# A two-layer convolution and GRU kernel: statistics of one image ahead of the blocks, the others beside them, and matrices built on four row tiles

## The chip, the cores and the metric

The kernel runs on one core of one Trainium2 chip. The time is device microseconds (us) of one execution. The engines of the core are TensorE (PE; PEld is its loading of weights), VectorE (DVE), ScalarE (ACT), GpSimd (POOL) and SyncE (SP). Each has its own queue of instructions[...]. DMAs are issued from the queues of SP, ACT and POOL.

## The reference, cut to what is computed

The input x is 4 images of 64 channels and 256 x 256 pixels in float32. Two layers follow each other, each on a normalised input (groups of two channels within an image) and with a residual.

```python
# layer 0
hidden = conv1x1(gn(x), w1); hidden = depthwise3x3(hidden, w_dw)
q, k, v = split(hidden, 3, axis=1)
out = irfft2(rfft2(patches8x8(q)) * rfft2(patches8x8(k)))
out = layernorm_over_channels(out) * ln_w + ln_b
x = x + conv1x1(v * out, w_out)
# layer 1: a GRU that walks over the 256 columns of gn(x)
x = x + gru_scan(gn(x), w_ih, w_hh, b_ih, b_hh)

def gn(v, G=32):      # mean and variance per image and group of 2 channels
    g = v.reshape(B, G, C // G, H, W)
    return ((g - mean(g)) / sqrt(var(g) + 1e-5)).reshape(v.shape)
```

The scalars of the first gn (one mean and one 1/sqrt(variance) for each image and group) need every pixel of that image before its first pixel can be normalised.

## The kernel before

It has four stages, all recorded through a small helper that keeps instructions in program order; so every instruction carries the helper's line, L156, in the profile, and tiles tell the groups apart.

**The start (lines 219 to 270).** Constants are loaded on ACT's queue. Then the matrices are built: depthwise convolution and transform together are linear, so for each of 384 hidden channels there is one matrix of 100 (a 10 x 10 patch with its border) by 64. It is a product of nine tap matrices (`bt`) with nine weights (`wd`): matmuls of 9 rows into PSUM (`psb`), in 16 groups of four with 256 columns and 16 groups of four with 128. ACT copies each group into the tile `t`, and POOL's queue writes three tiles to DRAM as `t_all`, 9.8 MB. Beside that, SP's queue loads x in 32 chunks `xc` of 2 MB, three buffers deep, and DVE takes eight `bn_stats` of 512 elements from each and aggregates them (`mv`). `group_norm_scalars` turns the means and variances of all images into `sc0`, with two small matmuls (against `avg`, which averages the two channels of a group), a Sqrt and sixteen copies.

**The blocks (lines 274 to 660).** 32 blocks `n`, eight to an image. For a block, POOL's queue loads the padded patches in four tiles `xq` of 800 KB (`load`), and `normalize` applies `sc0` of the image `n // 8` to them in place. Then in order:
- `pointwise(n, 0, ...)`: 16 units, each eight matmuls (`psring<-w_sb,xq`) and a copy into `h` by ACT, or by DVE for the units named in the call;
- `finish(n - 1)`: the gate, projection and residual of the block before, four units `u`; DVE adds the projection to the residual `xr` and takes `bn_stats` for layer 1, and SP stores `xr` in DRAM as `x1`. The last unit's projection is put off into the next step;
- `circular(n, 0, ...)`: for `sp` 0 to 3, `transform` of q and of k (64 matmuls `psring<-h,t`, the matrices `t` fetched by SP from `t_all`, four ahead), a copy of q by ACT, and the products `pr0`, `pr1` by DVE. After `sp` 2 an `inverse` (`psring<-pr,g_sb`) of the first two;
- `pointwise(n, 1, ...)`, `circular(n, 1, ...)` for the second half, beside which the layer norm of z (`layer_norm`, a generator advanced by `next(norm)`) takes its statistics on DVE;
- `pointwise(n, 2, ...)` and eight `values`, with `normalize` of block `n + 1`.

PSUM is one ring of eight banks (`psum()`), taken in turn. The work tiles q, k, pr0, pr1, y, xr and lnm share a pool `wk` of seven buffers: a tile gets a buffer that has come free and its first writer waits for the buffer's last readers.

**The turn to layer 1 (lines 667 to 681)** and **the GRU (683 to 836)** come last; the change touches only the load of `avg4` there.

Of the kernel before, what the change touches and what calls it, by code (L numbers as in the profile page):

```python
# [10 lines left out]
F32 = mybir.dt.float32  # L11
# [60 lines left out]
def tap_constants():  # L72
# [8 lines left out]
    return out.reshape(9, 128, HALO).astype(np.float32)  # L81


def group_norm_scalars(nc, pool, psum, avg, mv, eps, name):

    mean = pool.tile([P, NPAIR], F32, tag=f"{name}_mean", name=f"{name}_mean")
    rstd = pool.tile([P, NPAIR], F32, tag=f"{name}_rstd", name=f"{name}_rstd")  # L90
    m_c = pool.tile([P, NPAIR], F32, tag=f"{name}_mc", name=f"{name}_mc")
    d = pool.tile([P, NPAIR], F32, tag=f"{name}_d", name=f"{name}_d")
    nc.vector.tensor_copy(m_c, mv[:, :, 0])
    pm = psum.tile([P, NPAIR], F32, tag="gn", name=f"{name}_pm")
    nc.tensor.matmul(pm, lhsT=avg, rhs=m_c, start=True, stop=True)
    nc.vector.tensor_copy(mean, pm)
    nc.vector.tensor_tensor(d, m_c, mean, ALU.subtract)
    nc.vector.tensor_tensor(d, d, d, ALU.mult)
    nc.vector.tensor_tensor(d, d, mv[:, :, 1], ALU.add)
    pv = psum.tile([P, NPAIR], F32, tag="gn", name=f"{name}_pv")  # L100
    nc.tensor.matmul(pv, lhsT=avg, rhs=d, start=True, stop=True)
    nc.scalar.activation(rstd, pv, AF.Sqrt, bias=eps, scale=1.0)
    nc.vector.reciprocal(rstd, rstd)
    return mean, rstd
# [57 lines left out]
def tile_conv_then_gru(  # L162
# [26 lines left out]
    x_pair = x.rearrange("b c w h -> (b c) (w h)")  # L189
# [15 lines left out]

    wi = const.tile([P, 9, C], F32, tag="wi", name="wi")
# [11 lines left out]

    CH = 4096
    NST = W * H // 512  # L220
    with tc.tile_pool(name="xa", bufs=3) as xa, tc.tile_pool(name="sta", bufs=1) as sta, tc.tile_pool(
        name="gnps", bufs=1, space=PSUM
    ) as gnps, tc.tile_pool(name="bps", bufs=3, space=PSUM) as bps:
        avg = sta.tile([P, P], F32, tag="avg", name="avg")
        nc.scalar.dma_start(avg, avg2[0])
        wd = sta.tile([9, HID], F32, tag="wd", name="wd")
        nc.scalar.dma_start(wd, w_dw)
        ts = [sta.tile([HALO, P, NS], F32, tag=f"t{i}", name=f"t_{i}") for i in range(3)]
        for kind in range(2):
            bt = sta.tile([9, NS, HALO], F32, tag="bt", name=f"bt_{kind}")  # L230
            nc.scalar.dma_start(bt, taps[:, kind * NS : (kind + 1) * NS, :])
            for s in range(0, NS, 4):
                to = ts[0:2] if kind == 0 else ts[2:3]
                ps = bps.tile([HALO, 4, len(to) * P], F32, tag="b", name=f"psb_{kind}_{s}")
                for i in range(4):
                    nc.tensor.matmul(
                        ps[:, i, :],
                        lhsT=bt[:, s + i, :],
                        rhs=wd[:, 0 : 2 * P] if kind == 0 else wd[:, 2 * P : 3 * P],
                        start=True,  # L240
                        stop=True,
                    )
                for i, t in enumerate(to):
                    nc.scalar.copy(
                        t[:, :, s : s + 4], ps[:, :, i * P : (i + 1) * P].rearrange("p s c -> p c s")
                    )
        for i in range(3):
            nc.gpsimd.dma_start(
                t_all[i].rearrange("n p k -> p n k"), ts[i].rearrange("p (n c) k -> p n (c k)", n=8)
            )  # L250
# [641 lines left out]
```

## Time and profile before

| what | us |
|---|---|
| median of 3 runs (lowest, highest) | 5957.78 (5954.8, 5962.69) |
| the profiled execution, its own time | 5951.97 |
| its span, from first to last instruction | 5950.2 |
| first matmul of the blocks | 229.25 |
| issue of the four xq loads of block 0 | 215.66 |
| third write of t_all issued | 123.63 |
| first xq load of blocks 9, 10, 11 (one each block) | 1338.67, 1466.93, 1599.72 |
| busy: PE, DVE, ACT, POOL | 5537.8, 4085.5, 3465.8, 399.5 |

The three writes of `t_all` took 64.4, 80.3 and 114.1 us from issue to landing, while chunks of x were loaded beside them. In the profile a line of the timeline gives the start and the length in us, the engine, the operation, what it writes and reads with sizes, how many instructions of the kind were merged, and in brackets how long the engine had been idle and what ended that. In the rows of waits the numbers are us in total, how often, and the longest. "issue" is time in which the engine waited for nothing that the profile shows.

### The profile page before, as it was taken

To read this page: it belongs to the slowest core of one execution; us is meant where nothing else is said; L and a number is where in the kernel's file an instruction comes from. 1 tells how busy PE (TensorE), PEld (TensorE's weight loads), DVE (VectorE), ACT (ScalarE), POOL (GpSimd) and SP (SyncE) were. 2 spreads that over 40 slices of the span, in tenths; PEclk is the share of its full clock that TensorE was granted. 3 is DMA by queue.
4 is the path that set the end of the run, shared out by engine and by line. 5 is a ranking of instruction groups with operands and counts; after the bars stand their busy time and mean duration, and the time that the engine had idled before them with its cause. 6 is when DMAs were issued, how large, how long until landed. Compare 5 with 4: busy or idle time off the path is not lost.

```text
span 5950.2 us, 278865 instructions
## 1 busy us (share of the span) xinstructions
PE 5537.8 (93%) x127184; PEld 4770.7 (80%) x127184; DVE 4085.5 (69%) x9549; ACT 3465.8 (58%) x4617; POOL 399.5 (7%) x602
## 2 busy tenths in 40 slices
PE   5499999999999999999999999999979999999998
PEld 4478888888887888887888888888868888888887
DVE  7566776676676666676666767766666766676666
ACT  1256665666665656665565666565645555555555
POOL 0000000000000000000000000000002212122121
PEclk9999999999999999999999999999989999999999
DMA  9544545445445444444444554544444444444442
GB/s 384 213 133 144 139 132 147 121 141 144 140 126 142 137 135 141 140 134 133 143 124 138 146 144 123 149 131 132 128 119 113 113 113 113 113 112 113 111 113 80
DMA packets 549698, 817.79 MB, mean 137 GB/s; under 512 B 38443, under 2 KB 432436, under 8 KB 544404
## 3 DMA queue, kind: packets, MB, share of 16 engines
q1 hardware_dynamic: 523264, 683.80, 40.4%
q0 software_dynamic: 22320, 114.70, 5.8%
q8 instruction: 996, 16.32, 1.1%
q10 hardware_dynamic: 2934, 1.46, 0.1%
q14 instruction: 184, 1.51, 0.1%
HBM read 622.22 MB, written 144.05 MB: 129 GB/s over the span
## 4 chain that ended last, share of the span: by engine, by line
PE 64%; DVE 18%; ACT 7%; DMA 5%; issue 5%; SPq 0%; DVEq 0%; ACTq 0%; POOL 0%; POOLq 0%
PE psring L156 61%; DVE g L156 7%; DVE n L156 6%; DVE st L156 4%; ACT n L156 4%; DMA t<-t_all 2%; DMA xc<-in_x 2%; ACT v L156 2%; ACT z L156 1%; PE pshr L156 1%; PE pshz L156 1%; PE psni L156 1%; ACT h L156 1%; PE pshn L156 0%; SPq L156 0%
## 5 line engine op out<-in xcount | busy, mean ns | idle before, releaser
L156 PEld LDWEIGHTS psring<-h,t 100*32 100x32 f32 x40960 | 1336.1, 116 | 266.6 <-issue 184.8
L156 PE MATMUL psring<-h,t 100*32 100x128 f32 x40960 | 1437.4, 274 | 88.8 <-ACT h L156 35.6
L156 PEld LDWEIGHTS psring<-w_sb,xq 64*100 64x100 f32 x24576 | 1352.4, 163 | 86.1 <-issue 48.8
L156 PE MATMUL psring<-w_sb,xq 64*100 64x128 f32 x24576 | 1394.2, 271 | 27.3 <-POOL xq L156 17.8
L156 ACT COPY h<-psring 100x1024 f32<-100x1024 f32 x1274 | 1203.2, 1027 | 147.7 <-PE psring L156 140.9
L156 DVE TENSOR_TENSOR pr<-psring,q 128x512 f32<-128x512 f32 (+1 forms) x576 | 463.8, 860 | 338.6 <-PE psring L156 334.7
L156 DVE BATCH_NORM_STATS2 lnst<-z 128x6 f32<-128x64 f32 x4096 | 544.8, 212 | 118.7 <-ACT z L156 118.7
L156 DVE TENSOR_TENSOR z<-z,lnm 128x1024 f32<-128x1024 f32 x512 | 612.6, 1217 | 8.7
L156 ACT ACTIVATE n<-n,bias_sb 128x288 f32<-128x288 f32 (+7 forms) x510 | 259.8, 509 | 574.0 <-DVE n L156 574.0
L156 ACT COPY q<-psring 128x1024 f32<-128x1024 f32 x256 | 259.1, 1012 | 514.2 <-PE psring L156 457.6
L156 ACT COPY z<-psring 128x2048 f32<-128x2048 f32 x128 | 238.8, 1866 | 502.2 <-PE psring L156 485.1
L156 PE MATMUL psring<-pr,g_sb 32*64 32x512 f32 x8192 | 486.1, 598 | 7.2 <-issue 7.1
L156 ACT ACTIVATE y<-psring,ln_sb 128x512 f32<-128x512 f32 x512 | 372.1, 781 | 200.8 <-PE psring L156 197.2
L156 DVE COPY h<-psring 100x1024 f32<-100x1024 f32 x262 | 320.3, 1223 | 218.5 <-PE psring L156 216.2
L156 PE MATMUL pshr<-st,wi 64*64 64x144 f32 (+7 forms) x12240 | 433.3, 270 | 14.0 <-DVE st L156 13.4
L156 PE MATMUL psni<-st,wi 64*64 64x144 f32 (+7 forms) x12240 | 438.4, 270 | 8.0 <-issue 6.6
L156 DVE TENSOR_TENSOR g<-xn,n 128x288 f32<-128x288 f32 (+7 forms) x510 | 217.3, 426 | 325.2 <-ACT n L156 325.2
L156 PE MATMUL pshz<-st,wi 64*64 64x144 f32 (+7 forms) x12240 | 436.6, 269 | 1.8 <-issue 1.1
L156 DVE TENSOR_TENSOR y<-psring,y 128x1024 f32<-128x1024 f32 x256 | 312.3, 1220 | 122.7 <-ACT y L156 121.2
L156 POOL TENSOR_TENSOR raw<-raw,st 128x512 f32<-128x512 f32 x256 | 303.4, 1185 | 1208.1 <-DVE st L156 511.1
L156 PEld LDWEIGHTS pshr<-st,wi 64*64 64x64 f32 x12240 | 361.7, 133 | 17.0 <-issue 16.7
L156 PEld LDWEIGHTS psni<-st,wi 64*64 64x64 f32 x12240 | 361.5, 133 | 13.5 <-issue 9.9
(94 smaller groups left out, 6944.7 us busy)
## 6 DMA issues: line engine op xcount, KB each, us to landing
t<-t_all SPq DMA_DIRECT2D x768, 400.0 KB
xq<-in_xh POOLq DMA_DIRECT2D x128, 800.0 KB, 4.6
xc<-in_x SPq DMA_DIRECT2D x32, 2048.0 KB
xr<-in_x SPq DMA_DIRECT2D x256, 256.0 KB
x<-xr SPq DMA_DIRECT2D x256, 256.0 KB
raw<-x SPq DMA_DIRECT2D x128, 256.0 KB
raw<-x SPq DMA_DIRECT2D x256, 128.0 KB
xt<-xn SPq DMA_DIRECT2D x256, 128.0 KB
```

The source lines that it names most:

```text
L156: return self.tc.keep_in_program_order(got(*args, **kwargs))
```

## The change

The start takes the statistics of the first image only: eight chunks, each loaded as two halves of 64 partitions (`piece`: the image's upper and lower half of columns lie on the two halves of the partitions), with `bn_stats` into `bn0` and an aggregation into `st0` for each chunk. `norm_of_pieces` makes the scalars of one image from eight means and variances; it is a generator in three steps, and one matrix `avg2` serves everywhere.

In blocks 0 to 23 the next image is read in pieces beside the work: `look` loads 512 KB in two DMAs on POOL's queue into a work tile, `count` takes two `bn_stats` from it on DVE, four times in a block, and the fourth aggregates. In blocks 7, 15 and 23 `norm_of_pieces` is run at units 4, 8 and 12 of the third pointwise.

For the matrices, `bt` and `wd` are laid out on four groups of 32 partitions (nine rows of each used), so that the four matmuls of a group stand at four `tile_position`s and write four banks; ACT copies a group of 256 columns with one instruction. The loads of `wi`, `wh` and `bias_sb` stand after the scalars of the first image instead of ahead of everything.

```diff
-    avg = sta.tile([P, P], F32, tag="avg", name="avg")
...
+        bt = sta.tile([P, 32, HALO], F32, tag="bt", name="bt")
+        wd = sta.tile([P, HID], F32, tag="wd", name="wd")
+        for i in range(4):
+            nc.scalar.dma_start(bt[32 * i : 32 * i + 9], taps[i])
+            nc.sync.dma_start(wd[32 * i : 32 * i + 9], w_dw)
+        avg4 = sta.tile([P, 1024], F32, tag="avg4", name="avg4_0")
+        nc.sync.dma_start(avg4[:, 0:P], avg2)
+        ts = sta.tile([HALO, 3 * P, NS], F32, tag="ts", name="ts")
+        banks = bps.tile([P, 8, 512], F32, tag="b", name="psb")
+        for i in range(32):
+            kind, s = i // 16, i % 16
+            c0, num = 2 * P * kind, 2 * P - P * kind
+            ps = banks[0:HALO, 4 * (i % 2) : 4 * (i % 2) + 4, 0:num]
+            for k in range(4):
+                at = slice(32 * k, 32 * k + 9)
+                nc.tensor.matmul(
+                    ps[:, k],
+                    lhsT=bt[at, i, :],
+                    rhs=wd[at, c0 : c0 + num],
+                    start=True,
+                    stop=True,
+                    tile_position=(32 * k, 0),
+                )
+            nc.scalar.copy(ts[:, c0 : c0 + num, 4 * s : 4 * s + 4], ps.rearrange("p s c -> p c s"))
...
+        for i in range(8):
+            xc = xa.tile([P, 4096], F32, tag="xc", name=f"xc_{i}")
+            for at, of in piece(x, 0, i, 0, 16):
+                nc.sync.dma_start(xc[at], of)
+            for k in range(8):
+                nc.vector.bn_stats(bn0[:, k, :], xc[:, 512 * k : 512 * k + 512])
+            nc.vector.bn_aggr(st0[:, i, :], bn0)
+        for _ in norm_of_pieces(nc, st0, avg4, lambda: banks[:, 0, 0:1], eps, sc0[:, 0]):
+            pass
...
+def norm_of_pieces(nc, st, t, psum, eps, sc):
+    m_all, d, total, mean = t[:, 128:136], t[:, 136:144], t[:, 144:145], t[:, 145:146]
+    nc.vector.tensor_copy(m_all, st[:, :, 0])
+    nc.vector.tensor_reduce(total, m_all, mybir.AxisListType.X, ALU.add)
+    yield
+    pm = psum()
+    nc.tensor.matmul(pm, lhsT=t[:, 0:P], rhs=total, start=True, stop=True)
+    nc.vector.tensor_copy(mean, pm)
+    nc.vector.tensor_tensor(d, m_all, mean.to_broadcast([P, 8]), ALU.subtract)
+    nc.vector.tensor_tensor(d, d, d, ALU.mult)
+    nc.vector.tensor_tensor(d, d, st[:, :, 1], ALU.add)
+    nc.vector.tensor_reduce(total, d, mybir.AxisListType.X, ALU.add)
+    yield
+    pv = psum()
+    nc.tensor.matmul(pv, lhsT=t[:, 0:P], rhs=total, start=True, stop=True)
+    nc.scalar.activation(sc[:, 1:2], pv, AF.Sqrt, bias=eps, scale=1.0)
+    nc.vector.reciprocal(sc[:, 1:2], sc[:, 1:2])
+    nc.vector.scalar_tensor_tensor(sc[:, 0:1], mean, -1.0, sc[:, 1:2], ALU.mult, ALU.mult)
+    yield
...
+        def look(n, k, t):
+            for at, of in piece(x, n // 8 + 1, n % 8, 4 * k, 4):
+                nc.gpsimd.dma_start(t[at], of)
+
+        def count(n, k, t):
+            for i in range(2):
+                nc.vector.bn_stats(bn0[:, 2 * k + i, :], t[:, 512 * i : 512 * i + 512])
+            if k == 3:
+                nc.vector.bn_aggr(st0[:, n % 8, :], bn0)
...
-            circular(n, 0, lambda sp: None)
+            more = n // 8 + 1 < B
+            if more:
+                seen = work(f"seen0_{n}")
+                look(n, 0, seen)
+            circular(n, 0, lambda sp: count(n, 0, seen) if more and sp == 1 else None)
+            if more:
+                seen = work(f"seen1_{n}")
+                look(n, 1, seen)
             for unit in range(16):
                 pointwise(n, 1, unit, unit in (5, 8, 11, 14))
+                if more and unit in (8, 14):
+                    count(n, unit // 7, seen)
+                    look(n, unit // 7 + 1, seen)
             flush()
             norm = layer_norm(n)
-            circular(n, 1, lambda sp: next(norm))
+
+            def beside(sp):
+                next(norm)
+                if more and sp == 1:
+                    count(n, 3, seen)
+
+            circular(n, 1, beside)
+            image = None
+            if more and n % 8 == 7:
+                t = work(f"avg4_{n}")
+                nc.gpsimd.dma_start(t[:, 0:P], avg2)
+                image = norm_of_pieces(nc, st0, t, lambda: psum()[:, 0, 0:1], eps, sc0[:, n // 8 + 1])
             for unit in range(16):
                 pointwise(n, 2, unit, unit in (6, 14))
+                if image and unit in (4, 8, 12):
+                    next(image)
```

## The prediction

> **What bounds the kernel now.** I read the share of each engine over the whole span first, then stretches of the start, then the start and one block in order of time, and last what the TensorE (PE) waits for. The 40 slices:
>
> ```profile
> PE   5499999999999999999999999999979999999998
> DVE  7566776676676666676666767766666766676666
> DMA  9544545445445444444444554544444444444442
> ```
>
> After the first 1.5 slices (149 us each) PE is full until the end; DVE has about a third of its time free, but not evenly. At the start DMA is full and PE idle. Two stretches of the start (columns: busy us of PE, PEld, DVE, ACT, POOL; clock; DMA share; GB/s), then the timeline:
>
> ```profile
> 100.00:150.00 50.00, 22.72 (x107) 22.37 (x105) 41.95 (x65) 8.19 (x14) 1.00 (x1) 1.00 1.01 427
> 150.00:200.00 50.00, 0.00 (x0) 0.00 (x0) 38.69 (x65) 0.00 (x0) 0.00 (x0) 1.00 0.99 409
> ...
> 189.26 4.85 DVE L156 BATCH_NORM_STATS2 st<-xc 128x6 f32<-128x512 f32 x8 [1.42 <-DMA xc<-in_x]
> 200.68 4.84 DVE L156 BATCH_NORM_STATS2 st<-xc 128x6 f32<-128x512 f32 x8 [0.32 <-DMA xc<-in_x]
> 215.66 2.17 POOL L156 DMA_DIRECT2D xq<-in_xh  x4 [91.04 <-DMA t<-t_all]
> 229.25 6.51 PE L156 MATMUL psring<-w_sb,xq 64*100 64x128 f32 x64 [17.80 <-POOL xq L156]
> ```
>
> The reader sees: all 67 MB of x pass through DVE before the first useful matmul at 229.25 us, a chunk of 2 MB every 6.26 us (335 GB/s) while the matrices' writes share the DMA engines; a chunk costs DVE 4.85 us (0.605 us each of 8). From the issue of the xq loads to the first matmul it is 13.6 us. The statistics ahead of the blocks are thus the bound of the start, and PE of the blocks. In the steady part, from 1317 to 1445 us: products of a block's second half and its layer-norm statistics; then, in the next block, products of the first half around the residual of the block before, and a copy of the second pointwise stage:
>
> ```profile
> 1327.68 2.41 DVE L156 TENSOR_TENSOR pr<-psring,q 128x1024 f32<-128x1024 f32 x3
> 1346.31 5.46 DVE L156 BATCH_NORM_STATS2 lnst<-z 128x6 f32<-128x64 f32 x42
> ...
> 1410.07 2.42 DVE L156 TENSOR_TENSOR pr<-psring,q 128x1024 f32<-128x1024 f32 x3 [1.12 <-PE psring L156]
> 1412.41 1.28 DVE L156 TENSOR_TENSOR xr<-psring,xr 128x512 f32<-128x512 f32 x2
> 1415.56 2.42 DVE L156 TENSOR_TENSOR pr<-psring,q 128x1024 f32<-128x1024 f32 x3 [0.15 <-PE psring L156]
> 1419.06 1.23 DVE L156 TENSOR_TENSOR pr<-psring,q 128x1024 f32<-128x1024 f32 x1 [1.07 <-PE psring L156]
> 1437.42 1.23 DVE L156 COPY h<-psring 100x1024 f32<-100x1024 f32 x1 [1.40 <-PE psring L156]
> ```
>
> The brackets are DVE's slack: 1.12, 0.15 and 1.07 us around the first products, 1.40 us between pointwise copies, none at 1327.68. What PE waits for in blocks 1 to 30 (us in total, times, longest):
>
> ```profile
> PE psring L156 <- issue: 42.0, 40, 2.5
> PE psring L156 <- DMA t<-t_all: 7.6, 15, 1.0
> ```
>
> Fetches of the t matrices already come late now and then, so added DMA in the blocks isn't free.
>
> [...] in this trace the pointwise units, on two tiles of 64 rows, take 0.89 us for their eight matmuls of 128 columns (14.22 us for 16 units), so something does run side by side there.  [...] two queues share (335 GB/s of xc beside about 90 of t_all). [...]
>
> **The change part by part.**
>
> *Start.* Removed: 24 of 32 chunks of x. Left: 16.8 MB in 16 loads, 64 statistics and 8 aggregations. Those of 48 elements cost 0.37 us (the st<-bn row), so a chunk is 5.2 us of DVE. SP now issues four wd and one avg4 load first; I put the first chunk at 11 us. Eight chunks at 5.2 to 6.26 us end at 53 to 60 us, take 56. The new scalars have about ten DVE steps, two matmuls and a Sqrt instead of 13 more copies (209.22 to 215.25 took 6.0 us): 4.5 us, so 61 us.
>
> *Matrices.* bt now comes in four loads on ACT's queue behind five others; before, bt took 10.7 and 8.7 us to land under load. I take 19 us for the first matmul (14 to 22). Before, PE took 54.9 us for 16 groups of four 256-column matmuls and 27.6 us for 16 groups of 128 columns: 3.43 and 1.72 us a group. If four tiles run together it is a quarter, 0.86 and 0.43 us, and ACT is the slower: 1.03 us (the h row, of the same size) for 16 groups and 0.59 us (the t<-psb copies) for 16, 26 us in all. So the writes of t_all start at 36 and 45 us. Until 56 us they get 90 GB/s beside xc, about 1.8 MB of 9.8. The other 8 MB alone: [...] 20 to 30 us, so 76 to 86, take 80.5. xq (POOL) and the first t fetches wait for that landing and for the freed space, not for the statistics. Meanwhile ACT issues the 13 moved weight loads (0.65 us each plus lane waits, some 16 us before, 3.49 to 19.6) between 61 and 77, and b_rz on DVE waits for the last of them: hidden under the t_all writes; were those quicker, this would be next, at about 78. First matmul: 80.5 + 13.6 = 94 us. Gain 229.25 - 94 = 135 us, between 126 and 144.
>
> *Blocks 0 to 23, each.* Added: 8 loads of 256 KB on POOL's queue, 8 statistics (two take 1.29 us, bn<-xr row) and one aggregation, 5.5 us of DVE. Edit by edit:
> - Count 0, after the products of sp 1 (end 1417.98): 1.3 us into 1.07 us of idle; the products of sp 2 start 0.2 us late, and their bank is only needed by k of sp 3 after the inverse, over 2 us later. Nothing.
> - But the tile for it is one of the 7 work buffers. By the waits in the instruction order of the changed kernel, pr1 of sp 0 now gets the buffer whose last reader is the store of xr 2, which q of sp 1 got before. That store is issued at 1407.65 to 1408.9 and pr1 is due at 1411.3, 2.4 us later; all that the trace says of its landing is "before 1413.76". Delay of DVE 0 to 2.5 us, 1.4 taken; the inverse has 0.9 us of slack (1417.98 to 1418.93): 0.5 us lost, bounds 0 and 1.6.
> - Count 1 after the copy of unit 8: 1.3 in 1.40. Count 2 after unit 14: before 6.9 us of idle. Nothing. The load for count 2 starts when count 1 ends (1437.4) and is read at 1441.3 or, within that idle time, later[...]. POOL's queue holds behind these loads only xq loads, which are due later (1338.67 in the block shown).
> - Count 3 with the aggregation: 1.66 us into no idle at 1327.68, so the products end at 1331.75 instead of 1330.08; k of sp 3 on PE needs that bank after q of sp 3, at about 1331.75: 0.2 us lost.
> - DMA: 2 MB at 430 GB/s, 4.9 us of all engines per block, in four bursts, three beside transforms which prefetch t. Bounds 0 and 1.3 us (one burst in front of one fetch that has no slack), 0.5 taken.
> Sum 1.2 us, 29 us over 24 blocks; bounds 5 and 65.
>
> *Blocks 7, 15, 23.* The scalars' three steps stand in the third pointwise. The reading of the first matmul's result is in DVE's queue behind the 42 statistics (end 1351.77), and PE at unit 12 (about 1348.9) needs that bank and then the second matmul's operand, some five small DVE steps of 0.2 us later: PE waits 1348.9 to 1352.9, less the unit itself, 3.2 us. Three times: 10 us. PSUM's ring moves by four banks, which leaves its pattern alike.
>
> Sum: -135 + 29 + 10 = -96. The profiled execution took 5951.97 us (5950.2 span), giving 5856; the median of the runs shown stands 5.8 above it: 5862.
>
> **Rivals.**
> 1. All cover holds: matrices ready sooner (first matmul 86 us) and blocks pay 0.2 us each: -143 + 5 + 10 = -128, 5830. For it: DVE is idle a third of the time. Against: the fetches already late.
> 2. Half hidden: each block pays 3 us (store and fetches both on the path): -135 + 72 + 10 = -53, 5905. For it: DMA share 0.96 to 1.01 in the stretch 1404 to 1408, where the first look falls.
> 3. The four tiles don't overlap and the build doesn't do what it says: PE's 82.5 us replace ACT's 26, the third write starts at 101 us and ends at about 113 [...], first matmul 127: -102 + 39 = -63, 5895. For it: nothing here shows four tiles; against it: the two of 64 rows.
> 4. Slower: the store of xr 2, made of 512-byte pieces, [...] lands late, DVE's queue stands at pr1 of sp 0 and with it everything to the inverse. It decides from (135 - 10) / 24 = 5.2 us a block, a landing of 8.5 us after issue; the trace bounds it below 4.9 now. At 7 us a block: +43, 6001.
>
> **Numbers.** Forecast 0.66, rival 1 0.13, rival 2 0.08, rival 3 0.05, rival 4 0.06, and 0.02 for an end within 0.2% (12 us, what a measurement can tell from no change). Range 5826 to 5908: from rival 1 to rival 2 with their bounds. Faster 0.92, same 0.02, slower 0.06.
>
> **What would show it.** First w_sb,xq matmul at 86 to 103 us, released by the t_all landing, not by sc; a block of 24 lasting 129.3 us instead of about 128, the last eight unchanged; a PE wait of 3 us in blocks 7, 15, 23; DVE waiting for x<-xr at pr1. Wrong if xq waits for the statistics, or if PE waits for t grow by more than 2 us a block.

## The result and the profile after

| what | before | after |
|---|---|---|
| median (lowest to highest), 6 runs each, us | 5960.9 (5954.8 to 5975.34) | 5926.84 (5912.88 to 5938.16) |
| ratio, 95% interval | | 0.9938 [0.9926, 0.9951] |
| the profiled execution, its own time and span, us | 5951.97, 5950.2 | 5924.77, 5923.0 |
| first xq load, first matmul of the blocks, us | 215.66, 229.25 | 129.31, 140.37 |
| a block, mean of blocks 1 to 23, us | 129.07 | 130.86 |

The change is faster by 34 us (0.6 per cent) and not by the 96 us of the forecast's sum; 5926.84 lies above its range (5826 to 5908). Count a block from its first xq load to the next block's. Then the two spans compare piece by piece: the first xq load came 86.4 us sooner, block 0 took 2.8 us more, blocks 1 to 23 together 41.0 more, blocks 24 to 30 6.0 more, and what follows the first load of block 31 (its work, the turn to layer 1 and the GRU) 9.4 more. -86.4 + 2.8 + 41.0 + 6.0 + 9.4 = -27.2, the difference of the spans. Up to the first matmul of the blocks the start gave 88.9 us where 135 were forecast (140.37 us stands where 94 was expected), and everything behind it took 61.7 us more where 39 were forecast. The start is the larger part of the miss.

The page of after, three rows of the 40 slices:

```profile
PE   2999999999999999999999999999979999999998
DVE  2676776777667777776767776666766666676666
DMA  8455555555555555555555545444454444444442
```

The first digit of PE was 5 because the building of the matrices took long; now it is built quickly and PE stands idle for most of the slice all the same. DMA is at 5 instead of 4 in most slices of the blocks: the looks. Stretches of the start of after (columns: length, busy us of PE, clock, DMA share, GB/s):

```profile
20.00:30.00 10.00, 7.13 (x44) 1.00 0.96 202
40.00:50.00 10.00, 9.03 (x104) 1.00 1.02 215
80.00:90.00 10.00, 0.00 (x0) 1.00 1.01 286
110.00:120.00 10.00, 0.00 (x0) 1.00 0.68 187
120.00:128.00 8.00, 0.00 (x0) 1.00 0.28 68
```

The share and the bytes have to be read side by side. From 20 to 50 us the DMA engines are as busy as they were before, but they move 202 to 215 GB/s where the same share meant 409 to 427 GB/s before (from 100 to 200 us). At the end of the start they are busy for a quarter of their time only, and still neither PE nor DVE works. The timeline of after:

```profile
25.81 2.10 PE L157 MATMUL psb<-wd,bt 9*100 9x256 f32 x16 [0.25 <-ACT ts L157]
27.07 1.93 ACT L157 COPY ts<-psb 100x1024 f32<-100x1024 f32 x2 [0.40 <-PE psb L157]
27.67 0.37 DVE L157 BATCH_NORM_AGGREGATE st<-bn 128x2 f32<-128x48 f32 x1
37.01 0.37 DVE L157 BATCH_NORM_AGGREGATE st<-bn 128x2 f32<-128x48 f32 x1
...
54.94 1.00 POOL L157 DMA_DIRECT2D t_all<-ts  x1 [9.47 <-ACT ts L157]
...
97.48 0.37 DVE L157 BATCH_NORM_AGGREGATE st<-bn 128x2 f32<-128x48 f32 x1
...
128.52 7.54 SPq L157 DMA_DIRECT2D t<-t_all  x4
129.31 2.16 POOL L157 DMA_DIRECT2D xq<-in_xh  x4 [73.37 <-DMA wi<-in_w_ih]
140.37 5.21 PE L157 MATMUL psring<-w_sb,xq 64*100 64x128 f32 x64 [39.83 <-POOL xq L157]
```

An aggregation ends each chunk: they come about every 10 us, from 27.67 to 97.48, and DVE needs 4.84 us of that. So it is the loading that sets the pace now. The building runs well: two groups of four matmuls in 2.10 us, and the next two 2.32 us after them, with the two copies of ACT (1.93 us and a gap) as the pace: 1.16 us a group. The third write of `t_all` is issued at 54.94; from issue to landing the writes took 58.6, 81.7 and 73.5 us, while chunks of x were loaded beside them. The statistics and their scalars are done at 102.5, but the t fetch (SP's first loads of matrices from `t_all`) and the xq loads wait for the writes' landing: the third lands at 128.44. The bracket of the xq loads names a load of `wi`, because a wait for several things is put down to the one that came last. In a run below that loads `wi` much later, xq follows the landing just as closely (100.46 after 99.59 there, 129.31 after 128.44 here).

In the blocks, what PE waits for in after from 250 to 4100 us (us in total, times, longest):

```profile
PE psring L157 <- issue: 45.1, 49, 3.0
PE psring L157 <- DMA t<-t_all: 19.7, 30, 1.3
PE psring L157 <- DVE avg L157: 5.7, 3, 1.9
```

The same stretch of before has 39.0 us of issue, 7.6 us for t, and no avg. DVE in after, through blocks 1 to 23:

```profile
DVE pr L157 <- DMA x<-xr: 63.2, 23, 3.8
DVE bn L157 <- DMA seen<-in_x: 20.2, 23, 1.5
```

The first row is the wait that the prediction looked for at pr1 of sp 0: once a block, 2.75 us. The second is new too: a look that lands later than its count. The DMAs of the looks took 4.1 us to land in the median, where the prediction left 3.9 us or more between the start of the load for count 2 and its reading (1437.4 and 1441.3 us). Both are visible in the timeline of one block of after, block 9 from its first transforms on:

```profile
1342.93 1.29 DVE L157 TENSOR_TENSOR pr<-psring,q 128x512 f32<-128x512 f32 x2 [2.69 <-DMA x<-xr]
...
1350.80 2.42 DVE L157 TENSOR_TENSOR pr<-psring,q 128x1024 f32<-128x1024 f32 x3 [0.19 <-issue]
...
1372.13 1.29 DVE L157 BATCH_NORM_STATS2 bn<-seen 128x6 f32<-128x512 f32 x2 [0.74 <-DMA seen<-in_x]
...
1388.37 0.37 DVE L157 BATCH_NORM_AGGREGATE st<-bn 128x2 f32<-128x48 f32 x1
1388.66 2.35 DVE L157 TENSOR_TENSOR pr<-psring,q 128x1024 f32<-128x1024 f32 x3
```

DVE stands 2.69 us for the store of the residual, and yet PE's own waits for pr are 0.6 us in these 23 blocks: nearly all of it is slack, as far as the waits show.

### The profile page after: what moved, and what is told of

It reads as the page before. It is cut to its first block, busy times and chain, and to the rows that moved or that the text cites. A ratio compares the mean times of both kernels' runs of the same rounds, so it can differ in the third digit from the quotient of the medians.

```text
span 5923.0 us, 279366 instructions
## 1 busy us (share of the span) xinstructions
PE 5513.2 (93%) x127196; PEld 4736.6 (80%) x127196; DVE 4090.4 (69%) x9592; ACT 3466.3 (59%) x4604; POOL 499.7 (8%) x797
## 5 line engine op out<-in xcount | busy, mean ns | idle before, releaser
L157 PE MATMUL psring<-w_sb,xq 64*100 64x128 f32 x24576 | 1396.9, 271 | 58.1 <-POOL xq L157 44.1
L157 PE MATMUL pshr<-st,wi 64*64 64x144 f32 (+7 forms) x12240 | 434.0, 270 | 13.4 <-DVE st L157 12.9
L157 PEld LDWEIGHTS psni<-st,wi 64*64 64x64 f32 x12240 | 363.1, 133 | 14.3 <-issue 11.4
```

What stands on the lines that cost most here:

```text
L157: return self.tc.keep_in_program_order(got(*args, **kwargs))
```

## The experiments

Two things were to be settled: what holds the start, and what the looks cost in the blocks. For the start the first theory was that the halves of 64 partitions, in which the changed kernel loads each chunk, hold x at about half the rate; the rival was that the writes of `t_all` gate the blocks whatever x does. For the blocks the theory was the sum of the prediction (store, count, DMA, some 39 us); the rival was a part of it taking nearly all. Each timed run is compared with runs of the kernel before on the same chip.

### Chunks of 128 partitions, and blocks without looks

The first run loads the eight chunks in one DMA each, over all 128 partitions. A partition then holds half of a channel, so another averaging matrix (`avg1`) joins the four partitions of a group.

```diff
-            for at, of in piece(x, 0, i, 0, 16):
-                nc.sync.dma_start(xc[at], of)
+            nc.sync.dma_start(xc, x_flat[0:P, 4096 * i : 4096 * i + 4096])
```

> The changed kernel, but the eight chunks of the first image are loaded as one DMA of 128 partitions each (channel and half interleaved, with a matching averaging matrix), nothing else. Theory A (the two halves of 64 partitions hold the load of x at 200 to 215 GB/s): a chunk every 5.3 to 6.3 us instead of 10, statistics done near 60 to 65 us, first matmul of the blocks near 100 us instead of 140, time near 5887 us. Theory B (the writes of t_all are slow by themselves and gate the start): chunks quicker, but the first matmul stays above 130 us, time 5920 us or more.

Measured: 5894.0 us, ratio 0.9878 [0.9854, 0.9903]. The start of this kernel (columns as above):

```profile
20.00:30.00 10.00, 7.98 (x52) 1.00 0.98 411
50.00:60.00 10.00, 2.63 (x32) 1.00 1.00 365
70.00:80.00 10.00, 0.00 (x0) 1.00 0.94 260
80.00:90.00 10.00, 0.00 (x0) 1.00 0.70 211
90.00:100.00 10.00, 0.00 (x0) 1.00 0.28 72
```

From 20 to 30 us, at the same share, 411 GB/s instead of 202. The aggregations come every 5.29 us until 55.69, which is DVE's own time for a chunk (4.84 + 0.37 us and gaps), the last ends at 61.6, and the scalars are done at 66. First matmul: 113.13. That is the first part of the miss, 27 us of the start by these two profiles and 33 of the median, and the interval doesn't meet that of after. How far profiles of one start differ can be read from the other runs: this kernel and four below with the same start have the t fetch at 98.49 to 106.71 and the first matmul at 113.13 to 122.26, the three with halves (after and the two others in this part and the next) the first matmul at 140.37 to 144.04. So the halves cost 18 to 31 us of the start. The rival isn't dead, though: x is through at 61, and then the writes alone run at 249 to 260 GB/s and end in a tail; the t fetch stands at 98.49. The prediction had 80.5.

The second run keeps the halves at the start and leaves out every look and count; images 1 to 3 are normalised with the scalars of image 0.

```diff
-            more = n // 8 + 1 < B
+            more = False
```

> The changed kernel without the looks, counts and scalars of images 2 to 4 (these images take the scalars of the first; that part of the computation is left out). If the work put into the blocks costs what the two traces show between blocks 1 and 24 (1.8 us a block, 41 us in all): blocks of 129 us as in the kernel before, time near 5883 us, first matmul unchanged at 140 us. If the blocks vary by themselves and the added work is hidden: time near 5925 us.

Measured: 5889.9 us, ratio 0.9875 [0.9849, 0.9902], 37 us below after by the medians. A block takes 129.38 us on average (130.86 in after); DVE waits for the store 0.2 us in all, PE for t 8.5 us in blocks 1 to 23 (after 15.0, before 6.3). So all that the change put into the blocks costs about the 39 us that were forecast. The rest of what lies behind the start isn't looks: this kernel too takes 1783.4 us from the first load of block 31 on, as after does (1774.0 in before), and its blocks without looks are 0.3 us longer than those of before. The full kernel after also keeps one buffer instead of two for the tile `bn` of layer 1's statistics; DVE shows no wait for it here, and no run isolates it.

### The matrices alone, and the first look moved

The kernel before with the building on four tiles alone (`bt`, `wd` on four groups of 32 rows, statistics of all images first as before):

```diff
+            for k in range(4):
+                at = slice(32 * k, 32 * k + 9)
+                nc.tensor.matmul(
+                    ps[:, k],
+                    lhsT=bt[at, i, :],
...
+                    tile_position=(32 * k, 0),
```

> The kernel before with the four-tile building of the matrices alone (statistics of all images ahead of the blocks, as before). Theory A (the start of the kernel before is bound by loading x and the writes of t_all beside it): the building ends near 55 us instead of 123 us, the first matmul stays near 229 us, time within 0.2% of before. Rival (the building was on the path): first matmul 10 us or more earlier, time below 5950 us.

Measured: 5967.18 us, ratio 1.0006 [0.9995, 1.0017]. By itself it is worth nothing: the third write is issued at 66.33 us instead of 123.63, but all of x must still pass DVE before the first block, and the first xq load stands at 227.6 us (215.66 in before; why it is later in this profile isn't known). Built early is useful only if it is waited for.

Then the changed kernel with the first look put after the first transforms, its buffer taken there, and all four counts after these:

```diff
-            if more:
-                seen = work(f"seen0_{n}")
-                look(n, 0, seen)
-            circular(n, 0, lambda sp: count(n, 0, seen) if more and sp == 1 else None)
+            circular(n, 0, lambda sp: None)
...
-                if more and unit in (8, 14):
-                    count(n, unit // 7, seen)
+                if more and unit in (5, 11, 14):
+                    k = (5, 11, 14).index(unit)
+                    count(n, k, seen)
```

> The changed kernel with the first look taken after the first circular stage instead of before it, and the counts after units 5, 11 and 14; the work is the same, but no work buffer is held in the first circular stage. Theory A (DVE waiting at pr1 for the store of xr 2, 2.7 us in each of 23 blocks, is the larger part of the blocks' cost): that wait goes, blocks near 129.8 us instead of 130.9, time near 5900 us. Theory B (the DMA traffic beside the t fetches is the cost): the wait goes, the blocks stay within 0.4 us of 130.9, time near 5925 us.

Measured: 5970.13 us, ratio 1.0014 [0.9998, 1.003]: a miss, 43 us slower than after. The waits of PE and DVE of this kernel in blocks 1 to 23:

```profile
PE psring L157 <- DMA t<-t_all: 58.1, 61, 3.2
PE psring L157 <- issue: 32.1, 30, 4.1
```

```profile
DVE bn L157 <- DMA seen<-in_x: 112.8, 46, 5.0
```

The wait for the store is gone, as meant. But three looks now stand in one pointwise stage: each is issued only when the count before it has ended, so DVE stands for it (112.8 us instead of 20.2), and beside the t fetches PE waits 58.1 us for t instead of 15.0. A block takes 132.65 us. Removing the wait that shows most on DVE made the kernel slower, because DVE's wait was slack and the place of the DMAs was not. The granted TensorE clock (the mean share of full speed at which TensorE was let run) was lower as well, 0.985 to 0.990 over this kernel's runs and 0.991 to 0.992 over those of after, so the waits need not be the whole of the 43 us.

### The blocks, part by part

Three kernels, all with chunks of 128 partitions at the start and the scalars of image 0 for all images: looks in full with counts of 32 elements; counts in full on a constant, with no load and no buffer; buffers and loads of 64 elements a row, counts of 32.

```diff
-                nc.vector.bn_stats(bn0[:, 2 * k + i, :], t[:, 512 * i : 512 * i + 512])
+                nc.vector.bn_stats(bn0[:, 2 * k + i, :], t[:, 32 * i : 32 * i + 32])
```

> The kernel of e1_start128 with the looks as they are, but each count takes 32 elements instead of 512 a time, and images 2 to 4 take the scalars of the first (the statistics of these images are left out). It leaves the DMA and the work buffers of the change in the blocks and takes DVE's work away. Without any of it this start should give about 5857 us (5894 less the 37 us that the looks and counts cost together), blocks of 129.4 us. Theory A (DMA beside the t fetches, and the buffer that waits for a store, are the cost of the blocks): blocks of 130.2 us or more, time near 5885 us. Theory B (DVE's 5.5 us a block are the cost): blocks near 129.4 us, time near 5857 us.

```diff
-            for at, of in piece(x, n // 8 + 1, n % 8, 4 * k, 4):
-                nc.gpsimd.dma_start(t[at], of)
+            pass
...
-                seen = work(f"seen0_{n}")
+                seen = None
```

> The kernel of e1_start128 with the counts of 512 elements at their places, but reading a constant tile; no loads, no work buffer, and images 2 to 4 take the scalars of the first (the statistics of these images are left out). Theory A: blocks near 129.5 us, time near 5858 us. Theory B: blocks of 130.2 us or more, time near 5885 us.

```diff
-                nc.gpsimd.dma_start(t[at], of)
+                nc.gpsimd.dma_start(t[at, 0:64], of[:, 0:64])
```

> As e5_loads_in_blocks, but each look loads 64 elements a row instead of 1024, a sixteenth of the bytes (the statistics of images 2 to 4 are left out). It leaves the taking of a work buffer at the same places. If the wait of pr1 for the store of xr 2 comes from the buffer alone, DVE still waits some 2 us for that store in each of 23 blocks; if the loads slow the store, the wait falls below 1.5 us. If the buffers are the cost of the blocks, blocks of 130 us and 5875 us; if the bytes are, 129.4 us and 5857 us.

| kernel | us | ratio, 95% interval | block, us | DVE for the store, us a block | PE for t, us in 23 blocks |
|---|---|---|---|---|---|
| all (chunks of 128) | 5894.0 | 0.9878 [0.9854, 0.9903] | 130.53 | 2.8 | 13.4 |
| loads and buffers | 5883.08 | 0.9855 [0.9829, 0.9881] | 129.92 | 2.9 | 12.2 |
| buffers | 5873.36 | 0.9831 [0.9797, 0.9866] | 129.93 | 1.5 | 11.4 |
| counts | 5864.6 | 0.9820 [0.9791, 0.9849] | 129.72 | 0 | 9.0 |
| none (halves at the start) | 5889.9 | 0.9875 [0.9849, 0.9902] | 129.38 | 0.0 | 8.5 |

No part takes nearly all: against a block with none, counts cost 0.34 us, buffers 0.55, loads with buffers 0.54, all together 1.15 (in after 1.48), of which the image scalars, which the three kernels leave out, are 0.17. The profiles of five kernels with all looks and with chunks of 128 partitions lie between 130.53 and 131.09 us a block, and the TensorE clock granted in these blocks was 0.996 to 0.999 in the five profiles of the table, which is up to 0.4 us of a block if PE sets its pace (an estimate). So neither the order of these parts is shown nor that each of them costs; what is shown is that no single one is the sum. The wait for the store is 1.5 us with looks of a sixteenth of the bytes and 2.9 us when 2 MB of looks pass beside it.

A look as one DMA of 128 partitions was the last of this group:

```diff
-            for at, of in piece(x, n // 8 + 1, n % 8, 4 * k, 4):
-                nc.gpsimd.dma_start(t[at], of)
+            b, at = n // 8 + 1, 4096 * (n % 8) + 1024 * k
+            nc.gpsimd.dma_start(t, x_flat[b * P : (b + 1) * P, at : at + 1024])
```

> The kernel of e1_start128 with each look as one DMA of 512 KB over 128 partitions instead of two of 64 (all statistics are taken). If a load over half the partitions holds the DMA engines longer, as in the start, the waits of PE for t and of DVE for the store of xr 2 shrink: blocks near 130.0 us instead of 130.5, time near 5882 us. If only the bytes count: blocks of 130.5 us, time near 5894 us.

Measured: 5887.89 us, 0.9869 [0.9839, 0.9899]. DVE waits 6.8 us in all for looks (20.2 before), but a block takes 130.81 us, as with halves; against 0.9878 it is no difference that can be told.

### What holds the start when the halves are gone

With chunks of 128 partitions x is through at 61 us and the blocks begin at 113. Four runs turn to what lies between. First, `bt` and `wd` are loaded ahead of the constants of the blocks, so that building starts sooner:

```diff
-    hh_sb = const.tile([P, P], F32, tag="hh", name="hh_sb")
-    nc.scalar.dma_start(hh_sb, hh)
...
         for i in range(4):
             nc.scalar.dma_start(bt[32 * i : 32 * i + 9], taps[i])
             nc.sync.dma_start(wd[32 * i : 32 * i + 9], w_dw)
+        hh_sb = const.tile([P, P], F32, tag="hh", name="hh_sb")
+        nc.scalar.dma_start(hh_sb, hh)
```

> The kernel of e1_start128 with the loads of the taps and their weights ahead of the five constants on ACT's queue. If the landing of the writes of t_all gates the blocks (98.5 us in e1_start128), an earlier building moves it: first matmul of the building near 10 us instead of some 20, writes 8 us or more earlier, first matmul of the blocks near 104 us instead of 113, time near 5885 us. If the scalars or the loads of xq gate: 113 us and 5894 us still.

Measured: 5898.26 us, 0.9892 [0.9871, 0.9914]. The writes are issued at 37.04 and 48.76, 5 us sooner than in the run with chunks of 128, and take longer to land, 42.6 to 63.4 us instead of 35.0 to 44.3: the t fetch is at 104.29. That lies within the 98.49 to 106.71 of the five profiles with later taps, so the earlier building made no gain that shows. That the earlier writes only shared with x for longer is likely, but not shown.

On top of that, the GRU's weights loaded on POOL's queue in block 25 instead of after the first scalars:

```diff
-            nc.scalar.dma_start(wi[at, 3 * g : 3 * g + 3, :], w_ih[g].rearrange("t c o -> c t o"))
...
+            if n == 25:
+                for a in range(2):
+                    at = slice(a * C, (a + 1) * C)
+                    for g in range(3):
+                        nc.gpsimd.dma_start(wi[at, 3 * g : 3 * g + 3, :], w_ih[g].rearrange("t c o -> c t o"))
```

> The kernel of e8_taps_first with the 13 small weight loads of layer 1 moved from ACT's queue at the start to POOL's queue in block 25. If they only fill waiting time, first matmul as in e8_taps_first and the time within 6 us of it. If they hold up the last packets of t_all or the loads of xq, the first matmul comes 5 us or more earlier.

Measured: 5888.37 us, 0.9881 [0.9858, 0.9904]; t fetch 99.88, first matmul 114.46. The fetch is 4.4 us and the time 10 us ahead of the run before, but the two intervals overlap and the fetch lies within the spread of the five profiles. So it isn't shown whether the loads of the weights cost the writes something. In the next run the weights are back, the taps stay early, and the writes go on SP's queue behind x instead of on POOL's:

```diff
-            nc.gpsimd.dma_start(
+            nc.sync.dma_start(
                 t_all[i].rearrange("n p k -> p n k"),
```

> The kernel of e8_taps_first with the three writes of t_all on SP's queue, after the loads of x. If the writes are slow because of POOL's queue, they end earlier than in e8_taps_first, first matmul under 100 us. If 100 partitions spread badly over the engines on this queue, or if the queue keeps them behind x, they end later: first matmul 105 us or more.

Measured: 5900.88 us, 0.9901 [0.987, 0.9931]; t fetch 105.67. No gain shows from another queue. It isn't an equal comparison, though: behind x the third write was issued at 84.08 us only. Last, with early taps and the writes on POOL's queue, the first chunk alone is loaded, so that the writes have next to nothing beside them (seven eighths of image 0's statistics are left out):

```diff
-            xc = xa.tile([P, 4096], F32, tag="xc", name=f"xc_{i}")
-            nc.sync.dma_start(xc, x_flat[0:P, 4096 * i : 4096 * i + 4096])
+            if i == 0:
+                xc = xa.tile([P, 4096], F32, tag="xc", name=f"xc_{i}")
+                nc.sync.dma_start(xc, x_flat[0:P, 4096 * i : 4096 * i + 4096])
```

> The kernel of e8_taps_first with only the first of the eight chunks of the first image loaded (all eight statistics are taken from it; the rest of the image's statistics is left out). It shows the writes of t_all with next to nothing beside them. [...] 9.8 MB from about 30 us would land at 55 to 66 us, first matmul at 70 to 80 us. If they are slower by themselves (190 GB/s, as in e1_start128 between 61 and 98 us), they land at 80 us or more and the first matmul comes at 93 us or later.

Measured: 5871.5 us in a single run. This kernel's writes, alone (length, PE, clock, share, GB/s):

```profile
45.00:50.00 5.00, 1.93 (x24) 1.00 0.96 239
60.00:65.00 5.00, 0.59 (x2) 1.00 0.92 219
75.00:80.00 5.00, 0.00 (x0) 1.00 0.65 192
85.00:90.00 5.00, 0.00 (x0) 1.00 0.25 73
```

219 to 252 GB/s at a full share until 65 us, then a tail in which the share falls from 0.94 to 0.25. From the first issue at 36.3 to the last landing at 89.4 it is 53 us for 9.83 MB, 185 GB/s; the t fetch comes at 89.72, the first matmul at 103.63. That is the second part of the miss: with nothing in its way the write is slower than the 20 to 30 us that the prediction took for 8 MB; at 185 GB/s these are 43 us (an estimate).

### Why the writes alone are slow

Two causes were open: an uneven division of 100 partitions over the DMA engines, and the writes' short pieces (each partition writes eight pieces of 4 KB to places 400 KB apart). The expectations call the first theory D, the second F, and E that neither matters. With one chunk of x as in the last run, first each write is cut into 96 and 4 partitions:

```diff
-            nc.gpsimd.dma_start(
-                t_all[i].rearrange("n p k -> p n k"),
...
+            for at in (slice(0, 96), slice(96, HALO)):
+                nc.gpsimd.dma_start(
+                    t_all[i].rearrange("n p k -> p n k")[at],
```

> This is the kernel of the run with one chunk of x (the scalars of image 0 come from a chunk's worth of memory only, so the output differs), with each of the three writes of t_all cut into one of 96 partitions and one of 4. Theory D (100 partitions divide unevenly over the 16 DMA engines, so some finish early and the last 15 us run at a quarter of the share): the tail goes, the last landing comes 8 to 15 us sooner, the t fetch stands at 75 to 82 us instead of 89.7 and the first block matmul at 89 to 96 instead of 103.6. Theory E (the rate of a write is set by what each engine takes for a piece of 4 KB, whatever the cut): t fetch at 87 to 92 us, share over 0.9 at 219 to 252 GB/s as before.

Measured: t fetch 83.74, first matmul 98.51, so 6.0 us sooner for the fetch; 255 to 308 GB/s from 40 to 60 us, but the tail is there as before. The fetch falls between what D and E expected: the cut helped the rate and not the tail. Then `t_all` is laid out so that a partition's eight parts lie side by side in DRAM, one piece of 32 KB:

```diff
-    t_all = dram.tile([3, 8, HALO, 16 * NS], F32, tag="t_all", name="t_all")
+    t_all = dram.tile([3, HALO, 8, 16 * NS], F32, tag="t_all", name="t_all")
...
-                t_all[i].rearrange("n p k -> p n k"),
+                t_all[i],
```

> One chunk of x only, as in the first of these, and t_all kept in DRAM with the eight parts of a partition side by side, so that a write's piece is 32 KB long instead of 4 KB; the t fetches then read 4 KB pieces at a stride of 32 KB. Theory F (a write is slow because its pieces of 4 KB are short or are scattered in DRAM): share over 0.9 at 350 to 430 GB/s, t fetch at 70 to 78 us. Theories D and E: t fetch at 87 to 92 us, 219 to 252 GB/s as before.

Measured: landings after 16.6, 27.0 and 27.8 us instead of 30.6, 38.8 and 41.4. The stretches of this kernel, columns as above:

```profile
45.00:50.00 5.00, 2.08 (x24) 1.00 0.87 313
60.00:65.00 5.00, 0.58 (x2) 1.00 0.85 284
65.00:70.00 5.00, 0.00 (x0) 1.00 0.54 189
70.00:75.00 5.00, 0.00 (x0) 1.00 0.22 59
```

284 to 347 GB/s from 40 to 65 us, at a lower share; t fetch 77.33, first matmul 85.74. The fetch is where theory F had it, the rate a little below. So the layout of the pieces is the larger cause of the rate. It made them longer and put them side by side at once, and the run doesn't separate the two.

Short pieces are not slow in every company, however. The trace adds up the time that the packets of the three writes took on the DMA engines (packets, MB, share of 16 engines in the window). In before from 80 to 215 us, with one chunk of x from 36 to 90, and in long pieces from 36 to 76.5 it reads:

```profile
q0 software_dynamic: 3888, 9.84, 18.7%
q0 software_dynamic: 3888, 9.84, 72.4%
q0 software_dynamic: 384, 9.83, 69.3%
```

That is 404, 625 and 449 us of engine time. The same 4 KB pieces took 404 us with loads of x on 128 partitions beside them, less than the long ones alone. What makes them slower when they have the DMA engines to themselves is open. Spread evenly over 16 engines, the 625 us would last 39 us and the 449 us 28; the writes lasted 53 and 39.5, so the tail costs 11 to 14 us either way (an estimate).

The cause of the tail is not settled: it is there with the cut into 96 and 4 (shares of 0.64, 0.44 and 0.30 from 70 to 85 us) and with the long pieces (0.54 and 0.22 from 65 to 75), and no run here isolates it.

### In the whole kernel

The last four runs compute everything. Chunks of 128 partitions with the cut into 96 and 4:

> The changed kernel with the chunks of the start as 128 partitions, and t_all's writes cut 96 + 4. Theory D: first block matmul at 100 to 105 us instead of 113.1, the time 5881 to 5887 instead of 5894, ratio to before about 0.986. Theory E: 112 to 115 us and 5890 to 5897.

Measured: 5888.52 us, 0.9865 [0.9848, 0.9882]; t fetch 96.53, first matmul 109.89. Between D and E again; the fetch is ahead of the five profiles with whole writes, but the gain is too small to be told from 0.9878 in the times. Chunks of 128 partitions with the long pieces:

> The changed kernel with the chunks of the start as 128 partitions and t_all's writes in pieces of 32 KB, nothing left out. Theory F: the writes share with x until about 60 us and end some 10 us sooner than with 4 KB, so the t fetch stands at 84 to 92 us instead of 98.5, the first block matmul at 95 to 105 instead of 113, and the time is 5878 to 5888 instead of 5894. If the fetches of t at a stride of 32 KB cost in the blocks (768 fetches, PE waits for t now 15 us in all), the waits for t grow and the time stays at 5890 or more.

Measured: 5878.46 us, 0.9868 [0.9845, 0.9891]. The first xq load and the first matmul of this kernel:

```profile
88.49 2.13 POOL L157 DMA_DIRECT2D xq<-in_xh  x4 [32.88 <-DMA wi<-in_w_ih]
90.64 39.63 SPq L157 DMA_DIRECT2D t<-t_all  x8
96.56 5.68 PE L157 MATMUL psring<-w_sb,xq 64*100 64x128 f32 x64 [16.56 <-POOL xq L157]
```

The fetch, the first matmul and the time are in the range of theory F. Of the 16.6 us by which the first matmul is ahead of the run with 4 KB pieces, 10.6 are the earlier xq loads, and 6.0 are a shorter way from these to the matmul, possibly because they were issued ahead of the t fetches here and behind them there. The GRU's weights are now next in line: ACT issues the last of them until 93.73 and normalises the first xq, landed at 93.07, from 94.32. PE waits 13.9 us for t in the blocks (15.0 in after), so the fetches at a stride of 32 KB cost nothing that shows. Against this chip's runs of before (5957.43) the ratio is not apart from 0.9878, though, so the 16.6 us of the start are shown by the trace and not by the times. Next, all that looked good without the long pieces: chunks and looks of 128 partitions, late weights, the cut into 96 and 4:

> The same with each look as one DMA of 128 partitions and the GRU's weights loaded on POOL's queue in block 25. Looks of 128 gave 6 us and late weights some 5 us where each was alone, both about as large as their intervals, so 5876 to 5890 with theory D and 5882 to 5892 with theory E.

Measured: 5878.87 us, 0.9849 [0.9832, 0.9865], below after by 48 us and clear of it; first matmul 107.39. And the same with the long pieces:

> All that helped together: chunks and looks of 128 partitions, the GRU's weights in block 25, writes of 96 + 4 partitions in pieces of 32 KB. The 96 + 4 cut alone moved the t fetch by 6 us of the one-chunk run, the long pieces by 12; if they add, the t fetch stands at 80 to 88 us here and the time is 5865 to 5876, if the long pieces take it all 5870 to 5880 (5879 without them).

Measured: 5887.34 us, 0.9885 [0.9863, 0.9907]: a miss. The t fetch is at 93.16 and not at 80 to 88. The last chunk of x is aggregated at 81.32 us (61.86 in the run before, with 4 KB pieces; 76.94 with the long pieces alone), so the writes in long pieces take DMA time from x, and at the end comes the same tail: share 0.13 from 90 to 95 us. Gains that were measured one at a time on the same DMA engines did not add. The best two, at 5878 us, beat both kernels; which of the two is better isn't settled.

## Why the prediction was wrong

*Direction and mechanism* held: the statistics ahead of the blocks were the bound of the start of before, PE that of the blocks, the first xq loads waited for the landing of `t_all` and not for the statistics, and the cost in the blocks didn't eat the gain. The sizes of two terms of the start were wrong.

*Start, the chunk term ("Eight chunks at 5.2 to 6.26 us end at 53 to 60 us").* This is the first failed step. The rate came from loads of 128 partitions in the profile of before, and was carried over to pairs of loads of 64 without a price for that. They took 10 us a chunk at 202 to 215 GB/s, the statistics of the first began at 22.79 us where its chunk was put at 11, and the last aggregation ended at 97.85 us. The run with chunks of 128 partitions shows the price: from 20 to 30 us 411 GB/s for loads of 128 partitions, 202 for pairs of halves, at shares of 0.98 and 0.96. With loads of 128 partitions the last aggregation ended at 61.6, and the change gained 27 us more of the start (18 to 31 over the profiles) and 33 of the median.

*Matrices, the writes of t_all ("20 to 30 us, so 76 to 86, take 80.5").* The second failed step: the time of the other 8 MB alone was the author's estimate; no trace showed these writes alone. Alone, with pieces of 4 KB, the writes kept a share of 0.92 to 0.99 of all 16 engines at first, and yet they ran at 219 to 252 GB/s and had a tail, 185 GB/s over the whole; with 32 KB side by side the rate was 284 to 347. The profile of before could hardly have warned: beside x the same writes took 404 us of engine time, and spread over 16 engines that is 25 us or 390 GB/s (an estimate), by which 8 MB take 20.5 us, inside the prediction's 20 to 30. The writes also started later, at 43.23 and 54.94 us and not at 36 and 45. With both parts changed the first matmul stood at 96.56. Forecast 94, measured 140.37: of the 46 us between, 27.2 are the halves and 16.6 the layout of the pieces, in single profiles of starts that spread over 9 us. That 96.56 is so near to 94 is partly luck: the t fetch was at 90.64 and not at 80.5, and from xq to the first matmul it was 8.1 us and not 13.6.

*The rest of the start.* Four row tiles do work side by side: 3.43 us a group of 256 columns before, 1.16 after, so rival 3 falls. The first matmul of the building came at 13.30 us, but groups of four could follow each other only from 23.54, later than the 14 to 22 given, because the fourth part of `bt` landed then; the runs with earlier taps show no gain from mending that. Scalars took 4.7 us (4.5 forecast). The GRU's weights were hidden as far as ACT's queue goes: the last of them was issued at 130.65, and the first xq landed at 137.55. Whether their traffic slowed the writes is not shown. From xq to the first matmul it was 11.1 us (13.6 forecast).

*Blocks.* 1.2 us were forecast for each of 24, and 10 us for the three image blocks, 39 together. The run without looks puts them at 37 by the medians; against the profile of before, blocks 1 to 23 alone took 41.0 more where about 34 were forecast. By parts it was less exact. DVE's delay at pr1 is 2.75 us and not 1.4 (longest 3.8, over the bound of 2.5), though PE hardly pays for it; the waits for t rose by 8.7 us in 23 blocks, 0.38 each, where 0.5 was taken; the image blocks cost PE 1.9 us each and not 3.2. Counts 0 and 1, priced at nothing, may have cost more; 0.34 us a block for all counts is less than two profiles can tell. Rival 4, the late store, was far from its 5.2 us.

*Not forecast.* "The last eight unchanged" was off by 6.0 us in this profile: 1.9 are PE's wait for the scalars of the last image, which stands behind the first load of block 24, and 3.4 are waits for t (4.7 us instead of 1.3 between 3300 and 4100 us), whose cause stays open. What follows block 31's first load took 9.4 us more. It lasted 1774.0 to 1788.6 us in the profiles of the kernels here, though none changes the GRU's arithmetic, and the granted TensorE clock in it was 0.981 in the longest and 0.986 in the shortest. In before it was 0.986 and in after 0.983; if TensorE sets the pace there, that is an estimate of 6.5 of the 9.4 us. Why the clock differs is not shown.

## What to carry to other kernels

Read the DMA share and the GB/s together: here a share of 0.96 moved 202 GB/s in halves of 64 partitions where 0.98 moved 411 over 128, and writes in pieces of 4 KB moved 219 to 252 GB/s where 32 KB side by side moved 284 to 347. So carry a rate over only with the partitions and the pieces it was measured with. When a bound is taken away, price what was hidden behind it as it will then run, alone and with its shape: the same writes took 625 us of engine time alone and 404 beside loads of x. Before a difference of a few us between two starts is given a cause, see how far profiles of the same start lie apart: here it was 9 us. A wait on an engine off the critical path may be left where it is: with the first look moved, DVE's wait of 63.2 us for the store was gone and the kernel was 43 us slower.

## What the runs showed of the hardware

- From 20 to 50 us pairs of loads of 64 partitions moved 202 to 215 GB/s at a DMA share of 0.96 to 1.02, loads of 128 partitions 378 to 411 at 0.98 to 1.00 (from 43 and 42 us on with writes beside them).
- Writes from 100 partitions to DRAM moved 219 to 252 GB/s at a share of 0.92 to 0.99 in pieces of 4 KB, and 284 to 347 GB/s at 0.85 to 0.96 in pieces of 32 KB side by side. The 4 KB pieces took 625 us of engine time alone and 404 us beside loads of x.
- Each such set of writes ended in a stretch of 10 to 20 us at a falling share (0.25 in the last 5 us with pieces of 4 KB, 0.22 from 70 to 75 us with 32 KB), cut into 96 and 4 or not. Why is open.
- A store of the residual in pieces of 512 bytes landed 2.75 us later than DVE needed its buffer when looks passed beside it, 1.5 us with looks of a sixteenth of the bytes. Without looks, which take no buffer then, DVE hardly waited for a store (0.2 us in 23 blocks).
